# One weight chunk issued from ScalarE's queue, and two fewer warming products, at the start of a conditioned mixture-of-experts layer

## The chip, the cores and the metric

The kernel runs on one core of a Trainium2 chip. The metric is the device time of one execution in microseconds (us). The kernel before takes 261.87 us (median of 4 runs, 261.02 to 262.16).

## The reference

For 64 sequences of 64 rows of 512 values, a condition scales the rows, one layer follows, and then a base layer with a shared and a routed low-rank part; the input is added at the end. All is float32.

```python
# B=64 sequences, N=64 rows, D=512; condition q: (64, 256); E=6 experts of rank R=16, TOP_K=2
q_emb = relu(q @ W3 + b3)                              # (64, 512)
v     = (N * x + x.sum(axis=1, keepdims=True)) * q_emb[:, None, :]
y     = relu(v @ W2 + b2)

base   = y @ W_base + b_base
shared = (y @ A_s) @ B_s
gates  = softmax(y @ W_router + b_router)              # (…, 6)
w      = gates kept only at its TOP_K largest, else 0
routed = sum over e of ((y @ A_r[e]) * w[e]) @ B_r[e]
out    = x + base + shared + routed
```

## The kernel before

The 512 features lie on the partitions in four chunks of 128 (index `c`), the rows on the free axis. The 4096 rows are taken in four blocks (`k`) of 1024, each of two halves of 512 columns. In each block, the scaled input v goes through W2 (`py`, `yx`, `yy`, `yw`, `yz`, later `ia`, `ib`), then y through the concatenated low-rank and router weights (`ph`), then through W_base and the low-rank outputs (`ox`, `oy`, `oz`, `ow`, `last`). Most of the large products are written as Strassen-like sums of blocks, whose operand sums VectorE forms (`t`, `s`, `inner_t`, `tb`).

The order of instructions on each engine is the order of the source; there is no planner. Each engine has one queue, in order. DMAs are issued by SyncE's queue (SP), apart from two small stores at the very end that ScalarE issues (line 663).

What the change touches is the start of block 0:

- **Loads.** SP issues, in this order: `head` (condition, biases and W3's first output chunk, 198 KB, line 105), the first half of x's chunk 0 (`load_xa(0)`, 128 KB, line 100), W2's rows of chunk 0 (`load_w2(0)`, 256 KB, line 103), the second half of x's chunk 0 (`load_xa(1)`), the rest of W3 (384 KB, line 110), and then, for the chunks 1 to 3 in turn, x's first half (line 97), W2's rows, and the other half of x. The views call W3 and W2 together `w_sb`.
- **ScalarE's first instruction** is an activation of one column, `scratch` (line 106). Ahead of a kernel's first activation ScalarE loads its table of functions (ACT_TABLE_LOAD, shown under line 106).
- **TensorE's first instructions** are products of ones with ones in bf16 (`idle`, line 181): their result is never read. `first_mixed` runs eight, then the condition's product for output chunk 0 (`embed([0])`, `pq`, line 187), and two more products of ones.
- **The first scaled rows.** `embed` ends on ScalarE with the relu that gives `q_sb` (line 191). `modulate_group` works on VectorE: sums over each sequence (`vsum`, line 228), 64 x plus the sum (line 238, two instructions), times `q_sb` (line 242). The first quarter of block 0's chunk 0 then goes through W2 on TensorE (`part`, line 354, tile `py`, eight instructions), followed by `embed` for the three other chunks (twelve instructions) and then by the next quarter and the chunks 1, 2 and 3.
- **The second half of each chunk** is scaled on ScalarE (`modulate_scalar`, lines 247 to 250) and enters `yx` (line 361) and the sums of rows `s` (lines 263 to 266) that the products `yy`, `yw` and `yz` (line 170) take.

A float32 product is two instructions on TensorE in the views.

Of the kernel before, what the change touches and what calls it, by code (L numbers as in the profile page):

```python
# [15 lines left out]
P = 128  # L16
# [20 lines left out]
def adaln_ffn(ctx: ExitStack, tc: tile.TileContext, xa, x0, x1, head, w3, w2, wb, a, bcat, br, outT):  # L37
# [8 lines left out]
    nc = tc.nc  # L46
# [12 lines left out]
    def temps(name):  # L59

        return {n: tmp.tile([P, KH, TB], F32, tag=n, name=f"{n}_{name}") for n in pair_tags}

    def load_x(k):
        xs[k] = xpool.tile([P, NC, 2, TB], F32, tag="x", name=f"x_{k}")
        for c in CHUNKS:
            nc.sync.dma_start(xs[k][:, c].rearrange("p h t -> p (h t)"), x1[k, c])
# [24 lines left out]
    w2_sb = const.tile([P, NC, D], F32, tag="w2_sb", name="w2_sb")  # L91
# [7 lines left out]
    def load_xa(n):  # L99
        nc.sync.dma_start(xs[0][:, 0, ts(n, TB // 2)], xa[n])  # L100

    def load_w2(c):
        nc.sync.dma_start(w2_sb[:, c, :], w2[ts(c, P), :])

    nc.sync.dma_start(head_sb, head)
    nc.scalar.activation(scratch, ones[:, :1], AF.Relu)
    load_xa(0)
    load_w2(0)
    load_xa(1)
    nc.sync.dma_start(w3_sb, w3)  # L110
    for c in range(1, NC):
        load_x0(c, 0)
        load_w2(c)
        load_x0(c - 1, 1)
# [63 lines left out]
    def idle(n):  # L178
        p = ps_p.tile([P, TB], F32, tag="pp", name="idle")
        for _ in range(n):  # L180
            nc.tensor.matmul(p, ones[:, :P], ones, start=True, stop=True)

    def embed(fs, name):
        pq = ps_h.tile([P, len(fs), B], F32, tag="ph", name=name)
        for n, f in enumerate(fs):
            for c in range(NQ):
                nc.tensor.matmul(
                    pq[:, n], w3_of[f][:, c], cond_sb[:, c, :], start=(c == 0), stop=(c == NQ - 1)
                )
        for n, f in enumerate(fs):  # L190
            nc.scalar.activation(q_sb[:, f, :], pq[:, n], AF.Relu, bias=b3_sb[:, f : f + 1])
# [38 lines left out]
    def modulate_group(v, vsum, c, lo, hi):  # L230

        nb = hi - lo
        batch_sums(vsum, c, lo, hi)
        xc = batches_of(c, lo, hi)
        vc = v[:, c, :, lo * NH : hi * NH].rearrange("p h (b n) -> p h b n", n=NH)
        sc = vsum[:, c, lo:hi]
        for h in range(2):
            nc.vector.scalar_tensor_tensor(
                vc[:, h], xc[:, h], float(N), sc.unsqueeze(2).to_broadcast([P, nb, NH]), ALU.mult, ALU.add
            )  # L240
        q = q_sb[:, c, lo:hi].unsqueeze(1).unsqueeze(3).to_broadcast([P, 2, nb, NH])
        nc.vector.tensor_tensor(vc, vc, q, ALU.mult)

    def modulate_scalar(v, vsum, nq, c, lo, hi):

        batch_sums(vsum, c, lo, hi)
        nc.vector.tensor_scalar(nq[:, c, lo:hi], q_sb[:, c, lo:hi], float(N), None, ALU.mult)
        nc.vector.tensor_tensor(vsum[:, c, lo:hi], vsum[:, c, lo:hi], q_sb[:, c, lo:hi], ALU.mult)  # L248
        for b in range(lo, hi):
            nc.scalar.activation(  # L250
                v[:, c, :, ts(b, NH)], batches_of(c, b, b + 1)[:, :, 0], AF.Identity,
                bias=vsum[:, c, b : b + 1], scale=nq[:, c, b : b + 1],
            )

    def row_sums(a, name, cols=slice(0, TB)):

        all_s = mid.tile([P, 4, KH, TB], F32, tag=name, name=name)
        s = [all_s[:, i, :, cols] for i in range(4)]
        a11, a12, a21, a22 = a[:, :KH, 0, cols], a[:, KH:, 0, cols], a[:, :KH, 1, cols], a[:, KH:, 1, cols]

        def steps(c=slice(0, KH)):
            return [
                lambda: nc.vector.tensor_tensor(s[0][:, c], a21[:, c], a22[:, c], ALU.add),
                lambda: nc.vector.tensor_tensor(s[1][:, c], s[0][:, c], a11[:, c], ALU.subtract),
                lambda: nc.vector.tensor_tensor(s[2][:, c], a11[:, c], a21[:, c], ALU.subtract),
                lambda: nc.vector.tensor_tensor(s[3][:, c], a12[:, c], s[1][:, c], ALU.subtract),
            ]

        return {1: a11, 2: a12, 3: s[3], 4: a22, 5: s[0], 6: s[1], 7: s[2], "sums": all_s}, steps
# [3 lines left out]
    def fill(n):  # L273
        for _ in range(min(n, len(behind))):
            for step in behind.pop(0):
                step()
# [62 lines left out]
    def relu(y, f, h, src, cols=slice(0, TB)):  # L339
        nc.scalar.activation(y[:, f, h, cols], src, AF.Relu, bias=b2_sb[:, f : f + 1])  # L340

    def first_mixed(y):

        vs[0] = v = xpool.tile([P, NC, 2, TB], F32, tag="x", name="v_0")
        vsum = small.tile([P, NC, BB], F32, tag="vsum", name="vsum_0")
        nq = small.tile([P, NC, BB], F32, tag="nq", name="nq_0")
        half, cols = BB // 2, BB // 2 * NH
        other = slice(cols, TB)  # L350
        s, s_steps = row_sums(v, "s", other)

        def part(p, c, f, lo, hi):
            nc.tensor.matmul(  # L354
                p[:, :, lo * NH : hi * NH], w2_sb[:, c, ts(f, P)], v[:, c, :, lo * NH : hi * NH],
                start=(c == 0 and lo == 0), stop=(c == NC - 1), skip_group_check=True,
            )

        def without_sums(c):
            for j in range(KH):  # L360
                nc.tensor.matmul(  # L361
                    px[:, j], w2_sb[:, c, ts(j, P)], v[:, c, 0, other],
                    start=(c == 0 and j == 0), stop=(c % KH == KH - 1),
                    skip_group_check=True,
                )

        idle(8)
        embed([0], "pq0")
        idle(2)
        p0 = [ps_p.tile([P, 2, cols], F32, tag="pp", name=f"py_{f}") for f in range(NC)]  # L370

        px = ps_p.tile([P, KH, cols], F32, tag="pp", name="yx_0")
        p1 = mid.tile([P, KH, cols], F32, tag="p1", name="p1_0")
        for c in range(NC):
            pieces = ((0, half // 2), (half // 2, half)) if c == 0 else ((0, half),)
            for lo, hi in pieces:
                modulate_group(v, vsum, c, lo, hi)
                for f in range(NC):
                    part(p0[f], c, f, lo, hi)
                if c == 0 and lo == 0:  # L380
                    embed(range(1, NC), "pq")
            if c > 0:
                modulate_scalar(v, vsum, nq, c - 1, half, BB)
            if c == KH:
                for n in range(KH):
                    without_sums(n)
        nc.scalar.copy(p1, px)
        modulate_scalar(v, vsum, nq, NC - 1, half, BB)
        for f in range(NC):
            nc.scalar.activation(y[:, f, :, :cols], p0[f], AF.Relu, bias=b2_sb[:, f : f + 1])  # L390
        for c in range(KH, NC):
            without_sums(c)
        load_x(2)
        for step in t2_steps + inner_steps[:4] + s_steps():
            step()
        prepare(1, tb_steps + inner_steps[4:])
        fill(1)
        pairs = temps(0)
        for j in range(KH):
            relu(y, j, 0, px[:, j], other)  # L400
        banks = [ps_p.tile([P, KH, cols], F32, tag="pp", name=f"y{n}_0") for n in "ywz"]
        for j in range(KH):
            f1, f2 = j, KH + j
            temp = lambda n: pairs[n][:, j, :cols]
            py, pw, pz = (p[:, j] for p in banks)
            u, r, r1, r2 = temp("u"), temp("u22"), temp("u21"), temp("u12")
            product(py, 6, j, t2, s, start=j == 0)
            nc.vector.tensor_tensor(u, py, p1[:, j], ALU.add)
            product(pw, 5, j, t2, s, start=j == 0)
            nc.vector.tensor_tensor(r, pw, u, ALU.add)  # L410
            product(pz, 7, j, t2, s, start=j == 0)
            nc.vector.tensor_tensor(r, pz, r, ALU.add)  # L412
            relu(y, f2, 1, r, other)
            fill(1)
            product(pw, 3, j, t2, s, start=False)
            nc.vector.tensor_tensor(r2, pw, u, ALU.add)
            relu(y, f2, 0, r2, other)
            fill(1)
            product(pz, 4, j, t2, s, start=False)
            nc.vector.tensor_tensor(r1, pz, u, ALU.add)  # L420
            relu(y, f1, 1, r1, other)
            fill(1)
# [415 lines left out]
```

## Time and profile before

| | us |
|---|---|
| median of 4 runs (range) | 261.87 (261.02 to 262.16) |
| the profiled execution's own time | 261.66 |
| its span in the profile | 259.9 |
| TensorE busy (PE) | 254.9, 98% of the span |
| VectorE busy (DVE) | 193.8, 75% |
| ScalarE busy (ACT) | 136.5, 53% |
| GpSimd busy (POOL) | 38.7, 15% |
| bytes moved | 28.54 MB, mean 110 GB/s |

The span is the time from the first to the last record of the profiled execution; the execution's own time is 1.76 us longer. Starts are given in us from the start of the span. A busy share is an average over the whole span: the first microseconds, where the loads arrive, look different from the rest. PEld is TensorE's weight load, which overlaps with the products. "<-" in brackets names what ended the wait before an instruction.

### The profile page before, as it was taken

To read this page: it belongs to the slowest core of one execution; us is meant where nothing else is said; L and a number is where in the kernel's file an instruction comes from. 1 tells how busy PE (TensorE), PEld (TensorE's weight loads), DVE (VectorE), ACT (ScalarE), POOL (GpSimd) and SP (SyncE) were. 2 spreads that over 40 slices of the span, in tenths; PEclk is the share of its full clock that TensorE was granted. 3 is DMA by queue.
4 is the path that set the end of the run, shared out by engine and by line. 5 is a ranking of instruction groups with operands and counts; after the bars stand their busy time and mean duration, and the time that the engine had idled before them with its cause. 6 is when DMAs were issued, how large, how long until landed. Compare 5 with 4: busy or idle time off the path is not lost.

```text
span 259.9 us, 3177 instructions
## 1 busy us (share of the span) xinstructions
PE 254.9 (98%) x1004; PEld 164.5 (63%) x1004; DVE 193.8 (75%) x386; ACT 136.5 (53%) x373; POOL 38.7 (15%) x53
## 2 busy tenths in 40 slices
PE   7999999999999999999999999999999999999995
PEld 3756896454478888444458889544447889745453
DVE  2899898799968967968995894987895475872332
ACT  2399496596047896289017889349404428112000
POOL 1000000020017610002005630002001770000100
PEclk9999999999999999999999999999999999999999
DMA  6997639403320044000521024200332022400233
GB/s 210 381 342 261 268 105 374 166 3 121 121 81 0 13 154 161 0 3 2 199 82 42 0 83 164 81 0 3 121 121 81 0 79 89 159 0 3 75 140 108
DMA packets 14145, 28.54 MB, mean 110 GB/s; under 512 B 1472, under 2 KB 2496, under 8 KB 14128
## 3 DMA queue, kind: packets, MB, share of 16 engines
q1 hardware_dynamic: 13840, 28.21, 30.5%
q8 instruction: 8, 0.13, 0.2%
q10 hardware_dynamic: 288, 0.13, 0.2%
q14 instruction: 9, 0.07, 0.1%
HBM read 19.94 MB, written 8.39 MB: 109 GB/s over the span
## 4 chain that ended last, share of the span: by engine, by line
PE 94%; ACT 2%; DMA 2%; SPq 0%; issue 0%; DVE 0%
PE ia L446 13%; PE ph L779 11%; PE oz L170 11%; PE ox L170 11%; PE ib L446 10%; PE ow L170 9%; PE py L354 5%; PE oy L170 5%; PE ow L641 5%; PE ox L641 3%; PE oz L641 3%; DMA w_sb<-in_w_dram 2%; PE yw L170 1%; PE pt L704 1%; PE last L650 1%; PE yx L361 1%
## 5 line engine op out<-in xcount | busy, mean ns | idle before, releaser
L212 ACT ACTIVATE x<-x,vsum,nq 128x64 f32<-128x64 f32 x192 | 67.5, 431 | 7.0 <-DVE vsum L208 7.0
L779 PE MATMUL ph<-a_sb,y 128*128 128x118 f32 x256 | 30.5, 276 | 0.3 <-ACT y L340 0.3
L779 PEld LDWEIGHTS ph<-a_sb,y 128*128 128x128 f32 x256 | 30.0, 192 | 1.2 <-ACT y L340 0.7
L437 DVE TENSOR_TENSOR u<-ib,u 128x256 f32<-128x256 f32 x42 | 16.4, 418 | 18.5 <-PE ib L446 18.3
L452 ACT COPY ib<-ia 128x256 f32<-128x256 f32 x21 | 7.6, 361 | 42.3 <-PE ia L446 42.3
L170 PE MATMUL ox<-y,wb_sb 128*128 128x512 f32 x64 | 29.5, 593 | 0.0
L708 POOL TENSOR_TENSOR hwd<-hwT 112x512 f32<-112x512 f32 x4 | 5.8, 1452 | 136.3 <-ACT hwT L706 136.3
L170 PEld LDWEIGHTS ox<-y,wb_sb 128*128 128x128 f32 x64 | 11.9, 190 | 13.4 <-issue 13.2
L437 DVE TENSOR_TENSOR u<-ia,u 128x256 f32<-128x256 f32 (+1 forms) x36 | 16.1, 461 | 2.9 <-ACT u L484 1.6
L446 PE MATMUL ib<-inner_s,inner_t 128*128 128x256 f32 x60 | 17.8, 384 | 0.0
L340 ACT ACTIVATE y<-u,head_sb 128x256 f32<-128x256 f32 (+1 forms) x30 | 15.8, 585 | 3.8 <-DVE u L412 3.1
L637 DVE SCALAR_TENSOR_TENSOR xu<-oz,head_sb,xu 128x512 f32<-128x512 f32 x16 | 12.0, 749 | 7.2 <-PE oz L170 4.8
L207 DVE TENSOR_REDUCE vsum<-x 128x8 f32<-128x512 f32 x24 | 16.2, 675 | 0.0
L170 PE MATMUL oz<-sy,tb 128*128 128x512 f32 x32 | 15.2, 599 | 0.0
L170 PE MATMUL oz<-y,tb 128*128 128x512 f32 x32 | 15.1, 592 | 0.0
L170 PE MATMUL oy<-sy,tb 128*128 128x512 f32 x32 | 15.0, 592 | 0.0
L354 PE MATMUL py<-v,w_sb 128*128 128x512 f32 (+1 forms) x40 | 14.4, 510 | 0.6 <-DMA w_sb<-in_w_dram 0.6
L170 PE MATMUL ow<-sy,tb 128*128 128x512 f32 x28 | 13.2, 592 | 0.0
L170 PE MATMUL ow<-sy,wb_sb 128*128 128x512 f32 x28 | 13.2, 591 | 0.0
L455 ACT COPY ib<-ib 128x256 f32<-128x256 f32 x21 | 7.6, 363 | 9.9 <-PE ib L446 9.9
L446 PEld LDWEIGHTS ib<-inner_s,inner_t 128*128 128x128 f32 x60 | 11.2, 190 | 2.2 <-ACT ib L455 0.8
L250 ACT ACTIVATE v<-x,vsum,nq 128x64 f32<-128x64 f32 x32 | 11.0, 428 | 1.7 <-DVE vsum L248 1.7
(173 smaller groups left out, 461.9 us busy)
## 6 DMA issues: line engine op xcount, KB each, us to landing
xu<-in_x_dram SPq DMA_DIRECT2D x16, 512.0 KB, 4.3
out_dram<-xu SPq DMA_DIRECT2D x30, 256.0 KB, 2.0
x<-in_x_dram SPq DMA_DIRECT2D x12, 512.0 KB, 7.6
x<-in_x_dram SPq DMA_DIRECT2D x7, 256.0 KB, 5.4
w_sb<-in_w_dram SPq DMA_DIRECT2D x4, 256.0 KB, 5.3
wb_sb<-in_wb_dram SPq DMA_DIRECT2D x4, 256.0 KB, 5.0
w_sb<-in_w_dram SPq DMA_DIRECT2D x1, 384.0 KB, 4.9
out_dram<-xu SPq DMA_DIRECT2D x2, 192.0 KB, 1.9
```

What stands on the lines that cost most here:

```text
L170: nc.tensor.matmul(ps, w[i][:, c, ts(j, P)], s[i][:, c, :], start=start and c == 0, stop=c == KH - 1, skip_group_check=True,)
L207: nc.vector.tensor_reduce(vsum[:, c, bs], xc, AX.XY, ALU.add)
L212: nc.scalar.activation(x, x, AF.Identity, bias=vsum[:, c, b : b + 1], scale=nq[:, c, b : b + 1])
L250: nc.scalar.activation(v[:, c, :, ts(b, NH)], batches_of(c, b, b + 1)[:, :, 0], AF.Identity, bias=vsum[:, c, b : b + 1], scale=nq[:, c, b ...
L340: nc.scalar.activation(y[:, f, h, cols], src, AF.Relu, bias=b2_sb[:, f : f + 1])
L354: nc.tensor.matmul(p[:, :, lo * NH : hi * NH], w2_sb[:, c, ts(f, P)], v[:, c, :, lo * NH : hi * NH], start=(c == 0 and lo == 0), stop=(c = ...
L437: add = lambda o, a, b: nc.vector.tensor_tensor(o, a, b, ALU.add)
L446: nc.tensor.matmul(bank[b, t][:, cols], t_side(o, n), s_side(o, n), start=n == 1, stop=True, skip_group_check=True,)
L452: nc.scalar.copy(bank["b", t][:, lo], bank["a", t][:, lo])
L637: nc.vector.scalar_tensor_tensor(t, ps[name, j], bb_sb[:, f : f + 1], t, ALU.add, ALU.add)
L641: nc.tensor.matmul(ps[name, j], bcat_sb[:, ts(f, P)], hw, start=False, stop=True, skip_group_check=True)
L779: nc.tensor.matmul(ph[:, h * NS + s, :HC], y[:, c, h, ts(s, P)], a_sb[:, c, :], start=(c == 0), stop=(c == NC - 1),)
```

## The change

W2's chunk 0 is no longer issued third by SP. ScalarE's queue issues it, as its first instruction, ahead of the activation of `scratch` and so ahead of the table load. SP's other loads keep their order. The number of products of ones ahead of the condition's product goes from eight to six; the two behind it stay.

```diff
-    def load_w2(c):
-        nc.sync.dma_start(w2_sb[:, c, :], w2[ts(c, P), :])
+    def load_w2(c, queue=nc.sync):
+        queue.dma_start(w2_sb[:, c, :], w2[ts(c, P), :])
 
     nc.sync.dma_start(head_sb, head)
+    load_w2(0, nc.scalar)
     nc.scalar.activation(scratch, ones[:, :1], AF.Relu)
     load_xa(0)
-    load_w2(0)
     load_xa(1)
...
-        idle(8)
+        idle(6)
         embed([0], "pq0")
         idle(2)
```

## The prediction, written before the change was run

> **What bounds the kernel now.** I read the page first, then the chain of waits in order of time, then the timeline of the first 16 us, then single tiles. The page's chain says which engine carries the span:
>
> ```profile
> PE 94%; ACT 2%; DMA 2%; SPq 0%; issue 0%; DVE 0%
> ```
>
> TensorE carries it, so a gain at the start survives only if TensorE still has it when it later meets another engine with no slack. The start of the chain (start, length, what):
>
> ```profile
> 0.74 0.38 SPq L105
> ...
> 1.18 0.42 SPq L100
> ...
> 1.64 4.48 DMA w_sb<-in_w_dram
> ...
> 6.26 1.96 PE py L354 x8
> 8.22 1.28 PE pq L187 x12
> ```
>
> The first products on x (py) start at 6.26, released by W2's first chunk: issued third on SP's queue at 1.64, landed at 1.64 + 4.48 = 6.12. The change aims at this. The timeline (start, length, engine, line) shows what is late next:
>
> ```profile
> 0.73 1.28 ACT L106 ACT_TABLE_LOAD   x1 [0.73 <-PEq L824]
> 0.77 3.57 PE L181 MATMUL idle<-const-bfloat16-1.0 128*128 128x512 bf16 x8 [0.77 <-PEq L824]
> ...
> 3.61 0.42 DVE L228 TENSOR_REDUCE vsum<-x 128x4 f32<-128x256 f32 x1 [3.61 <-DMA x<-in_xa_dram]
> 3.71 1.19 PEld L187 LDWEIGHTS pq<-head_sb 128*128 128x128 f32 x4 [0.28 <-issue]
> ...
> 4.14 0.95 PE L187 MATMUL pq<-head_sb 128*128 128x64 f32 x4
> ...
> 5.13 0.31 ACT L191 ACTIVATE q_sb<-pq,head_sb 128x64 f32<-128x64 f32 x1 [2.90 <-PE pq L187]
> ...
> 5.47 0.42 DVE L242 TENSOR_TENSOR v<-v,q_sb 128x256 f32<-128x256 f32 x1 [0.92 <-ACT q_sb L191]
> ...
> 8.14 0.69 DVE L228 TENSOR_REDUCE vsum<-x 128x8 f32<-128x512 f32 x1 [0.22 <-DMA x<-in_x_dram]
> ...
> 9.54 0.72 ACT L191 ACTIVATE q_sb<-pq,head_sb 128x64 f32<-128x64 f32 x3 [4.11 <-PE pq L187]
> 9.89 0.69 DVE L242 TENSOR_TENSOR v<-v,q_sb 128x512 f32<-128x512 f32 x1 [0.27 <-ACT q_sb L191]
> ```
>
> The scaled x (v) is ready at 5.47 + 0.42 = 5.90, only 0.22 before W2. It hangs on the condition's product (4.14), which stands behind the eight products of ones. From 8.14 on VectorE hardly rests; its one wait there is 0.27 at 9.89, for q_sb from products that come after py. Does VectorE have slack later? The timeline around 24 us:
>
> ```profile
> 24.94 1.10 PE L170 MATMUL yy<-s,t 128*128 128x256 f32 x4
> ```
>
> Those products need the sum of L264, which VectorE starts at 24.10 and ends 0.69 later, at 24.79. Slack is about nothing, so what reaches the end is what VectorE gains at 9.89.
>
> **The change part by part.**
>
> *ScalarE's queue.* W2's issue takes some 0.42 (SP's rows at 1.18 and 1.64) ahead of the table load: the load moves from 0.73 to 1.16 and ends at 2.44, the activation of `scratch` (0.20) at 2.64. ScalarE's next work is at 5.13; this costs nothing while those 2.5 us cover it. Without that cover it would cost 0.42.
>
> *SP's queue.* Every SP issue behind the head chunk and the first half of xa moves up by one place, 2.11 - 1.64 = 0.47. Whether the landings follow is open, because the engines are 93 to 104% busy from 2 to 8 us (346 GB/s at 4 to 6): bounds 0 and 0.47. The ones that matter are x at L228 (wait 0.22, landed 8.12) and W3 (issued 2.58, 4.9 to land, 7.4 to 7.5, used at 7.84). Call this d2; I take at least 0.1, toward the low end, since a busy engine gains nothing from an earlier issue.
>
> *W2 itself.* Issued at 0.73 with the same 4.48 it lands at 5.21; with the 198 KB of the head beside it, 198/346 = 0.57 later, 5.78. Either is before 5.90.
>
> *The head chunk.* It now shares the DMA engines with W2's 256 KB: delay d1 between 0 (head first) and 256/346 = 0.74 (W2 first), as far as bytes go. The trace's packet records add a far end: W2's first packets took 0.33 to 0.66 on eleven occasions and 1.3 and 1.6 on two, where 0.084 is usual, so the ceiling is 0.74 + 1.60 = 2.34. I take 0.37, the middle of the byte bounds, because two queues of about equal size are likely to take turns. The first half of xa may be delayed likewise, but its reduce and two following steps end at 4.55 and L242 starts at 5.47: 0.92 of cover.
>
> *Six products of ones.* They start every 0.427, so two free 0.85; but the head lands at 0.74 + 2.5 = 3.24 (3.28 for its last part), so the weight load at 3.71 can move only to about 3.28 + 0.11 = 3.39 (0.11 is what lay between W2's landing and the load after it). Its first product stood 0.43 behind it because the last product of ones was still running; unobstructed, 0.15 to 0.33. The condition's product moves by 0.42 to 0.60; I take 0.50, before d1.
>
> *The clock.* The weight loads of the condition take 333 ns until 4.57 and 190 ns from 6.33; the trace's clock record has the full clock from 5.16, though the page's row of the clock shows 9 in every slice. Fewer ones leave TensorE a gap of about (3.39 + d1) - 3.33 ahead of the condition. I cost it at nothing: the two products of ones behind the condition, and a gap of 0.64 that the kernel already had at 5.62, lie around it. If the step to full clock is missed, the eight py products double from 1.73 to 3.46.
>
> Sum. The condition moves 0.50 - 0.37 = 0.13 earlier: v at 5.77, py at 5.77 + 0.14 = 5.91 instead of 6.26, a gain of 0.35. The weights of the twelve pq products load 1.58 after py (7.84 against 6.26), so at 7.49; W3, at 7.4 with d2 = 0.1, does not hold them. So q_sb at 9.54 and L242 at 9.89 gain 0.35 if x lets them: L228 can give 0.27 + d2, enough from d2 = 0.08. After that VectorE, ScalarE (back to back from 17.44) and TensorE at 24.94 move by the same 0.35. In the profiled execution's own time: 261.66 - 0.35 = 261.31. That execution lies 0.21 under the median of 261.87, so against the median 261.5.
>
> Two rules speak against more. The Trainium skill, "DMA: Bandwidth & Descriptors", section "Issuing engines are not separate DMA queues", says that transfers from different issuing engines run on the same 16 DMA engines, so a second queue saves only issue time. By that rule the gain in bytes is zero (d2 = 0, a gain of 0.27) where my bounds have 0 to 0.47; no row here shows SP's and ScalarE's loads sharing at the start. "TensorE: Matmul & The Clock Gate", Part 1, says that the clock is released by a free-running window of 3.4 us of activity, not by a count of products; by it a missed window would hold py at half speed and cost up to 1.7, against my zero.
>
> **The rivals.**
>
> *A, the head comes first and all issues count (faster).* d1 = 0 moves the condition by 0.42 to 0.60, v to 5.30 to 5.48, py to 5.44 to 5.62: 0.64 to 0.82. L242 follows if d2 is 0.45 or more, that is if nearly all of the 0.47 reaches the landings. Time 261.87 - 0.75 = 261.1. For: W2's wait does end last at 6.26. Against: DMA engines at 93 to 104%.
>
> *B, the head stands behind W2 on the DMA engines (slower).* Place: the landing of head_sb, which gates the product at 4.14. From d1 = 0.50 + 0.22 = 0.72 on, py starts later than now, and each further us goes one for one through q_sb (no slack at 9.89). With W2's bytes first (0.74) and a slow packet of about 1 us, d1 is 1.74 and the loss 1.0: 262.9. The ceiling of 2.34 loses 1.6: 263.5. It passes 0.3% when the head lands after 3.28 + 1.51 = 4.8. TensorE then also idles over 1.5 us before the clock step. For: W2's slow first packets, now beside the head. Against: SP's head issue is no later than ScalarE's.
>
> *C, the table load still goes first.* Then W2 is issued at 2.02 or later, lands from 6.50, py starts at 6.64: 0.4 lost, 262.3.
>
> **How the numbers follow.** Forecast 0.34, A 0.29, B 0.32, C 0.05. A difference of 0.3% (0.79 us) is about what a measurement of this kernel can tell from no change: 261.08 to 262.66. The forecast's own range is 261.1 to 261.9 (d1 from 0 to 0.74 at a move of 0.50: gain 0.72 to 0), all inside the 0.3%. A straddles the border: 0.25 faster, 0.04 inside. B: 0.30 slower, 0.02 inside. C is inside. Together 0.25 faster, 0.45 same, 0.30 slower. The range for 8 in 10 reaches down to 260.7 (A's best, 261.87 - 0.82 = 261.05, less about 0.35, since single runs of before stand between 0.85 under and 0.29 over their median) and up to 262.9, which leaves out the upper half of B.
>
> **What would show it.** Right: a first packet of W2 before 2 us on ScalarE's queue, the condition's first product at 3.9 to 4.1, py at 5.8 to 6.0 released by VectorE and no longer by W2, L242 of the second chunk at 9.5 to 9.6, the products on s at 24.6. Wrong: a reduce of the first half of xa after 4.3, a condition's product after 4.6 released by the head (B), weight loads of 333 ns still in py (a missed clock), or L228 at 8.1 with the wait of 9.89 gone (x as the bound, gain at most 0.27).

## The result

The changed kernel takes 262.73 us in the median of 54 runs (261.26 to 263.57); before takes 261.64 in 78 runs over the same time. The ratio is 1.0031, with a 95% interval of 1.0024 to 1.0039: slower, by about the 0.3% that the prediction named as the border. The means are 262.52 and 261.69, 0.82 apart; the medians lie 1.09 apart. The median hides the shape. The 54 times fall into two groups with nothing between 261.77 and 262.32: 13 runs from 261.26 to 261.77, and 41 from 262.32 to 263.57. The 78 runs of before lie in one group up to 262.28, apart from two at 263.6.

The profiled execution of the change, 263.57 us with a span of 261.8, belongs to the upper group. Its page's chain still lies on TensorE:

```profile
PE 94%; ACT 2%; DMA 1%; DVE 1%; issue 0%; SPq 0%; DVEq 0%
```

The start of the chain of waits (start, length, what) no longer holds W2:

```profile
0.74 0.37 SPq L105
...
1.16 3.86 DMA x<-in_xa_dram
...
6.59 3.48 PE py L354 x8
10.06 1.28 PE pq L187 x12
```

W2 has left, and the first half of xa stands in its place. But py begins at 6.59 (6.26 before), and the same eight products take 3.48 us instead of 1.96. The timeline (start, length, engine, line, what, and in brackets the wait) shows the steps between:

```profile
0.73 0.41 ACTq L103 DMA_DIRECT2D w_sb<-in_w_dram  x1
...
0.77 2.72 PE L181 MATMUL idle<-const-bfloat16-1.0 128*128 128x512 bf16 x6 [0.77 <-PEq L824]
...
1.17 1.28 ACT L107 ACT_TABLE_LOAD   x1 [1.17 <-PEq L824]
...
4.41 1.12 PE L187 MATMUL pq<-head_sb 128*128 128x64 f32 x4 [0.92 <-DMA head_sb<-in_head_dram]
...
5.05 0.42 DVE L228 TENSOR_REDUCE vsum<-x 128x4 f32<-128x256 f32 x1 [5.05 <-DMA x<-in_xa_dram]
...
5.56 0.31 ACT L191 ACTIVATE q_sb<-pq,head_sb 128x64 f32<-128x64 f32 x1 [2.89 <-PE pq L187]
6.11 0.43 DVE L242 TENSOR_TENSOR v<-v,q_sb 128x256 f32<-128x256 f32 x1
...
6.59 3.48 PE L354 MATMUL py<-v,w_sb 128*128 128x256 f32 x8 [0.21 <-DVE v L242]
...
11.39 0.72 ACT L191 ACTIVATE q_sb<-pq,head_sb 128x64 f32<-128x64 f32 x3 [5.51 <-PE pq L187]
11.73 0.69 DVE L242 TENSOR_TENSOR v<-v,q_sb 128x512 f32<-128x512 f32 x1 [2.50 <-ACT q_sb L191]
```

The six products of ones are through at 3.49, the head chunk lands at 4.36 (3.28 before), and TensorE waits 0.92 us for it. The first half of xa lands late too, at 5.02 instead of 3.58, and it sets the start of py: q_sb is ready at 5.87, but L242 starts only at 6.11, 1.06 behind the start of xa's reduce, and this distance is 1.05 to 1.07 in every profile with W2 on ScalarE's queue. The L242 that decides is at 11.73 instead of 9.89, and the products on s behind it are late by the same amount:

```profile
26.77 1.10 PE L170 MATMUL yy<-s,t 128*128 128x256 f32 x4
```

26.77 - 24.94 = 1.83 of the 1.91 by which the two profiled executions differ (263.57 - 261.66). Of these, 0.33 is the later start of py and 3.48 - 1.96 = 1.52 its length. The view of the tile `w_sb` up to 12 us says why py is long (duration in ns as min/median/max):

```profile
L354 PEld LDWEIGHTS py<-v,w_sb x13: 190/338/338, 6.6 to 11.9; 128*128 128x128 f32 x13
```

These weight loads took 190 in the py of before; 338 is what they take at the lower clock (333 in the condition of before, ahead of the step). The trace's record of the clock gives full speed from 9.62 on, where the profile of before has 5.16. TensorE stepped up late and did nearly all of py at the lower clock, half of full speed by that record.

So there are two suspects, which came together: the clock (a rest of TensorE, a stretch without any product, ahead of the condition's product makes it miss the step: theory 1), and the bytes (the head and xa land late because W2 shares the DMA engines with them: theory 2). The products of ones might also count by their number (theories 3 and 4).

### The profile page after: what moved, and what is told of

It reads as the page before. It is cut to its first block, busy times and chain, and to the rows that moved or that the text cites. A ratio compares the mean times of both kernels' runs of the same rounds, so it can differ in the third digit from the quotient of the medians.

```text
span 261.8 us, 3173 instructions
## 1 busy us (share of the span) xinstructions
PE 256.3 (98%) x1002; PEld 165.2 (63%) x1002; DVE 193.7 (74%) x386; ACT 136.5 (52%) x373; POOL 38.7 (15%) x53
## 4 chain that ended last, share of the span: by engine, by line
PE 94%; ACT 2%; DMA 1%; DVE 1%; issue 0%; SPq 0%; DVEq 0%
PE ia L446 13%; PE ph L779 11%; PE oz L170 11%; PE ox L170 11%; PE ib L446 10%; PE ow L170 9%; PE py L354 6%; PE oy L170 5%; PE ow L641 5%; PE ox L641 3%; PE oz L641 3%; DMA x<-in_xa_dram 1%; PE yw L170 1%; PE pt L704 1%; PE last L650 1%; PE yx L361 1%
## 5 line engine op out<-in xcount | busy, mean ns | idle before, releaser
L354 PE MATMUL py<-v,w_sb 128*128 128x512 f32 (+1 forms) x40 | 15.9, 555 | 0.2 <-DVE v L242 0.2
L354 PEld LDWEIGHTS py<-v,w_sb 128*128 128x128 f32 x40 | 8.5, 218 | 6.7 <-issue 4.8
```

What stands on the lines that cost most here:

```text
L354: nc.tensor.matmul(p[:, :, lo * NH : hi * NH], w2_sb[:, c, ts(f, P)], v[:, c, :, lo * NH : hi * NH], start=(c == 0 and lo == 0), stop=(c = ...
```

## Experiments

**One half of the change each, and a gap without the queue.** The first keeps W2 on ScalarE's queue with eight products of ones; the next two keep SP's queue with six and with four.

```diff
# e1_queue_only, against the change        # e2_six_only (e3_four_only: 4), against before
-        idle(6)                             -        idle(8)
+        idle(8)                             +        idle(6)
```

> W2's first chunk on ScalarE's queue as in the change, but eight products of ones as before. Theory 1 (the clock: the 0.92 us in which TensorE waits for the head is what makes it miss the step to the full clock): the eight products end at 4.2 instead of 3.3, the wait for the head shrinks to some 0.2 us, the clock steps up before the products py in nearly all executions, and the time is 261.2 to 261.6, 0.998 to 1.000 of before. Theory 2 (the bytes: the head lands 1.1 us late, and everything behind it is late): the head still lands at about 4.4, and the time stays at 262.5 to 263, 1.003 to 1.005 of before.

> W2's first chunk on SyncE's queue as before, six products of ones. Theory 1 (the gap before the condition): the head lands at 3.3 as the six products end, the gap is about 0.1 us, no step of the clock is missed, and the condition's product comes some 0.4 us earlier but py still waits for W2 at 6.1: 261.4 to 261.7, 0.999 to 1.001. Theory 3 (the number of products of ones by itself): as the change, 262.5 to 263, 1.003 to 1.005. Theory 2 (late bytes): no loss, as theory 1.

> W2's first chunk on SyncE's queue as before, four products of ones: the products end at 2.5 and the head lands at 3.3, so TensorE waits some 0.9 us ahead of the condition, as after the change, while every DMA is as before. Theory 1 (the clock): most executions miss the step and lose 1.0 to 1.7 us: 262.3 to 263.3, 1.003 to 1.006. Theory 2 (late bytes): no loss, 261.4 to 261.7, 1.000.

| | median us (range, runs) | ratio to before (95%) |
|---|---|---|
| e1, ScalarE's queue, eight | 261.45 (261.39 to 261.79, 11) | 0.9987 (0.9978 to 0.9995) |
| e2, SP's queue, six | 262.83 (261.18 to 263.54, 12) | 1.0024 (1.0006 to 1.0042) |
| e3, SP's queue, four | 262.73 (262.32 to 263.69, 7) | 1.0038 (1.0022 to 1.0053) |

The queue alone is faster, in one narrow group. Six products alone are as slow as the change, with no DMA touched. Theory 2 expected the reverse in both. But theory 1 in the form I gave it missed e2 too: I had looked only at the rest ahead of the condition. The timeline of e2, TensorE alone:

```profile
3.28 1.05 PE L187 MATMUL pq<-head_sb 128*128 128x64 f32 x4
4.12 1.06 PE L181 MATMUL idle<-const-bfloat16-1.0 128*128 128x512 bf16 x2
6.18 3.75 PE L354 MATMUL py<-v,w_sb 128*128 128x256 f32 x8 [0.99 <-DMA w_sb<-in_w_dram]
```

There is no rest ahead of the condition, as I expected; the rest has moved behind it, 0.99 us until W2 lands. The clock steps up at 10.14 and py takes 3.75. In e3 the rest ahead of the condition is 0.61, and the step comes at 8.33. In e1, by contrast (TensorE, and VectorE's L242 that decides):

```profile
4.14 0.91 PE L187 MATMUL pq<-head_sb 128*128 128x64 f32 x4
4.88 0.60 PE L181 MATMUL idle<-const-bfloat16-1.0 128*128 128x512 bf16 x2
5.93 1.99 PE L354 MATMUL py<-v,w_sb 128*128 128x256 f32 x8 [0.45 <-DVE v L242]
...
9.60 0.69 DVE L242 TENSOR_TENSOR v<-v,q_sb 128x512 f32<-128x512 f32 x1 [0.67 <-ACT q_sb L191]
```

The head lands at 3.80 here, while the eight products still run; the condition starts at 4.14 as before, the clock steps up at 4.88, and py starts at 5.93 instead of 6.26, released by VectorE.

**W2 behind the table load.**

```diff
# e4_after_table, against the change
-    load_w2(0, nc.scalar)
     nc.scalar.activation(scratch, ones[:, :1], AF.Relu)
+    load_w2(0, nc.scalar)
```

> W2's first chunk on ScalarE's queue, but behind the table load and the activation of scratch, six products of ones. Its issue moves to about 2.2, so its packets no longer stand beside the head's. Theories 1 and 2 alike: the head lands at 3.3 to 3.5, no gap, the clock steps up in time; W2 lands between 5.2 and 6.3, and the time is 261.2 to 261.8, 0.998 to 1.000. If the head is late here too (two queues sharing is not its cause), 262.5 or more.

262.68 us (261.45 to 263.54, 12 runs), ratio 1.0028 (1.0009 to 1.0047). The expectation failed at its first step. The timeline:

```profile
0.73 1.28 ACT L106 ACT_TABLE_LOAD   x1 [0.73 <-PEq L824]
...
0.79 0.38 ACTq L103 DMA_DIRECT2D w_sb<-in_w_dram  x1
```

ScalarE's sequencer issued the DMA at 0.79, during the table load ahead of it; only the engine was held. "Ahead of the table" in the change is therefore worth 0.06 us, and e4 is the change over again: the head at 3.65, six products, the clock's step at 9.33. It does not tell whether W2 causes the head's delay.

**The same number of products in other places.**

```diff
# e5_six_four, against before              # e6_queue_six_four, against the change
-        idle(8)
+        idle(6)                                     idle(6)
         embed([0], "pq0")                           embed([0], "pq0")
-        idle(2)                             -        idle(2)
+        idle(4)                             +        idle(4)
```

> W2's first chunk on SyncE's queue as before; six products of ones ahead of the condition and four behind it (before: eight and two). Theory 1 (rests of TensorE inside one window of the clock's monitor): the two moved products fill the rest of about 1 us that six alone left between the condition and py; TensorE works nearly without a rest from 0.8 to 5.8, the clock steps up by 7.6 at the latest, 261.2 to 261.8, 0.998 to 1.001. Theory 3 (the number of products ahead of the condition): slow as with six and two, 262.5 to 263.3, 1.002 to 1.006.

> W2's first chunk on ScalarE's queue; six products of ones ahead of the condition and four behind it. The total of ten is that of before, but the rest of some 1 us ahead of the condition, while TensorE waits for the head, stays. Theory 1 (rests): most executions still miss the step, 262.4 to 263.6, 1.002 to 1.006 (the two added products can also put py back by up to 0.4). Theory 4 (the total number of products of ones before py): 261.3 to 261.9, 0.998 to 1.001.

| | median us (range, runs) | ratio to before (95%) |
|---|---|---|
| e5, SP's queue, six and four | 261.66 (261.16 to 262.76, 12) | 0.9999 (0.9984 to 1.0013) |
| e6, ScalarE's queue, six and four | 263.01 (261.37 to 263.67, 12) | 1.0035 (1.0015 to 1.0056) |

Both kernels run ten products of ones, six of them ahead. On SP's queue the four behind fill the rest; on ScalarE's queue TensorE waits ahead of the condition, where they cannot help. TensorE in the timelines, first of e5 and then of e6:

```profile
3.29 1.12 PE L187 MATMUL pq<-head_sb 128*128 128x64 f32 x4
4.21 1.33 PE L181 MATMUL idle<-const-bfloat16-1.0 128*128 128x512 bf16 x4
5.42 1.97 PE L354 MATMUL py<-v,w_sb 128*128 128x256 f32 x8
```

```profile
3.82 1.12 PE L187 MATMUL pq<-head_sb 128*128 128x64 f32 x4 [0.33 <-DMA head_sb<-in_head_dram]
4.73 1.91 PE L181 MATMUL idle<-const-bfloat16-1.0 128*128 128x512 bf16 x4
6.44 2.92 PE L354 MATMUL py<-v,w_sb 128*128 128x256 f32 x8
```

e5 has no rest and steps up at 4.80; e6 rests 0.33 by the records, less than the 1 us expected, and steps up at 8.51. Neither the number ahead (theory 3) nor the total (theory 4) decides: it is where TensorE rests.

**Between six and eight, and one more behind.** Both against the change: e7 runs eight and three, e8 seven and two.

```diff
# e7_queue_eight_three, against the change # e8_queue_seven, against the change
-        idle(6)                             -        idle(6)
+        idle(8)                             +        idle(7)
         embed([0], "pq0")                           embed([0], "pq0")
-        idle(2)                                     idle(2)
+        idle(3)
```

> W2's first chunk on ScalarE's queue; eight products of ones ahead of the condition, three behind it. Theory 1: the rest of 0.45 ahead of py, which the kernel with eight and two on this queue still had, is filled too; no step is missed, 261.2 to 261.6, 0.997 to 0.999. If the third product comes in py's way where the clock is still at half speed, up to 0.3 is lost again, 261.5 to 261.8.

> W2's first chunk on ScalarE's queue; seven products of ones ahead of the condition, two behind it. The rest ahead of the condition is between those of six (1.1) and eight (0.2 or less): some 0.1 to 0.6 as the head lands at 3.8 to 4.4. Theory 1: a mixture, some executions miss the step; the median lies between 261.4 and 262.6 and single ones reach from 261.2 to 263.3. Theory 2 (late bytes alone): one group of times, spread as before.

e7: 261.45 (261.37 to 261.81, 12 runs), ratio 0.9984 (0.9975 to 0.9993). e8: 261.51, with ten runs from 261.35 to 261.63 and two at 263.16 and 263.45, ratio 0.9996 (0.9979 to 1.0014). Seven products give a mixture, with fewer slow runs than six. e7 is level with e1 within the intervals. The added product did not fill the rest: in e7's profile py still waited 0.58 for VectorE, since xa landed at 4.53 and the step at 4.48 had shortened the added product. It bought nothing that these runs can tell from e1.

**The same kernel in both groups.** The change itself, three more single runs, each with its profile, beside a run of before at 261.47:

> The change itself once more, one look, to find an execution of the lower group of its times (13 of 54 executions lie at 261.3 to 261.8). Theory 1 (the clock): in such an execution the step to the full clock comes before 8.6 us, py takes about 2 us and not 3.5, and the time is 261.3 to 261.9; in one of the upper group the step comes after 8.6 and py takes 3 us or more. Theory 2 (late bytes): the groups differ in the landing of the head, and not in the clock.

> As the look before this one: the same kernel once more, with the same two groups of times and the same expectation of each theory for either group.

> As the two looks before this one: the same kernel once more, with the same two groups of times and the same expectation of each theory for either group.

They took 263.36, 261.59 and 262.95 us. The first two in the timeline, TensorE alone and then TensorE with the steps that release py:

```profile
4.05 1.12 PE L187 MATMUL pq<-head_sb 128*128 128x64 f32 x4 [0.55 <-DMA head_sb<-in_head_dram]
4.96 1.06 PE L181 MATMUL idle<-const-bfloat16-1.0 128*128 128x512 bf16 x2
6.12 3.73 PE L354 MATMUL py<-v,w_sb 128*128 128x256 f32 x8
```

```profile
4.04 0.66 PE L187 MATMUL pq<-head_sb 128*128 128x64 f32 x4 [0.55 <-DMA head_sb<-in_head_dram]
4.54 0.60 PE L181 MATMUL idle<-const-bfloat16-1.0 128*128 128x512 bf16 x2
4.56 0.42 DVE L228 TENSOR_REDUCE vsum<-x 128x4 f32<-128x256 f32 x1 [4.56 <-DMA x<-in_xa_dram]
...
4.74 0.31 ACT L191 ACTIVATE q_sb<-pq,head_sb 128x64 f32<-128x64 f32 x1 [2.07 <-PE pq L187]
...
5.62 0.42 DVE L242 TENSOR_TENSOR v<-v,q_sb 128x256 f32<-128x256 f32 x1
...
6.10 1.99 PE L354 MATMUL py<-v,w_sb 128*128 128x256 f32 x8 [0.96 <-DVE v L242]
```

In both, the head lands at 4.00, the rest is 0.55 and py starts within 0.02 us. The clock's step is at 9.66 in the one and at 3.54 in the other, py takes 3.73 or 1.99, and the times are 1.77 apart: 3.73 - 1.99 = 1.74 of it is py. Theory 2 is out as the cause of the two groups.

The third, 262.95, lies between them, and its step does too, at 8.81:

```profile
6.08 3.33 PE L354 MATMUL py<-v,w_sb 128*128 128x256 f32 x8
```

At half speed, half of the time from the start of py to the step is lost. That is (9.66 - 6.12) / 2 = 1.77 in the first and (8.81 - 6.08) / 2 = 1.37 in the third; against the second, their times are 1.77 and 1.36 longer. So the step's time accounts for the place within the upper group as well.

**What the profiles say of the clock's rule.** The clock's full-speed stretch is recorded as 256.00 or 252.59 us in each of the 13 profiles, and these differ by 3.41, a 75th of 256.00: the step goes by windows of 3.41 us. This is the window that the Trainium skill names ("TensorE: Matmul & The Clock Gate", Part 1), which it calls free-running, and the steps here do come at another phase in each execution. How full must the last window before the step be? Counting back 3.41 from each step, by TensorE's records:

| profile | time us | window that gave the step | rest in it | window before it | rest |
|---|---|---|---|---|---|
| before | 261.66 | 1.75 to 5.16 | 0.00 | | |
| e1 (eight) | 261.39 | 1.47 to 4.88 | 0.00 | | |
| e5 (six and four, SP) | 261.64 | 1.39 to 4.80 | 0.00 | | |
| e7 (eight and three) | 261.56 | 1.07 to 4.48 | 0.00 | | |
| e8 (seven) | 261.53 | 0.76 to 4.18 | 0.07 | | |
| change, second single run | 261.59 | 0.13 to 3.54 | 0.70 (0.65 at its start) | | |
| change | 263.57 | 6.21 to 9.62 | 0.21 | 2.80 to 6.21 | 0.92 |
| change, first single run | 263.36 | 6.25 to 9.66 | 0.00 | 2.84 to 6.25 | 0.66 |
| change, third single run | 262.95 | 5.39 to 8.81 | 0.10 | 1.98 to 5.39 | 0.51 |
| e2 (six, SP) | 263.54 | 6.73 to 10.14 | 0.00 | 3.32 to 6.73 | 0.99 |
| e3 (four, SP) | 262.40 | 4.91 to 8.33 | 0.44 | 1.50 to 4.91 | 0.61 |
| e4 (six, behind the table load) | 263.16 | 5.92 to 9.33 | 0.21 | 2.51 to 5.92 | 0.46 |
| e6 (six and four) | 262.83 | 5.10 to 8.51 | 0.00 | 1.69 to 5.10 | 0.33 |

Windows with no rest or little of it step up, and those with 0.92 or more do not. In between, the time of rest alone does not decide: 0.70 was enough in the second single run, where everything else was products of ones, and 0.44 in e3, but 0.33 was too much in e6. Every window in the last column also holds products of the condition, with 64 columns. That short products count for less would explain it; it was not tried by itself.

The phase explains the two groups. Six products of ones make a stretch of 2.7 us, and only a window that covers nearly all of it steps up in time; the next one ends 3.41 later. Where the border lies can be estimated. The shortest time of the upper group is 0.91 above the middle of the lower one (262.32 against 261.41), so its step came at about 6.1 + 2 x 0.91 = 7.9, in a window that followed one started at about 1.1. The window of the second single run started at 0.13 and stepped up; one of e2's that started at -0.10, just before the first record, did not. By this estimate windows that start between about 0.1 and 1.1 give the lower group, 1.0 of 3.41 or 29% of the phases if all are equally likely (not shown); 13 of 54 runs (24%) were in it.

With eight products there is hardly a rest after 0.77 as long as the clock is low. The condition starts at 4.14, and by the rows of the change the two products behind it start 0.91 later and take 1.06 at the lower clock, until 6.11; py follows at 6.26 in before. This is an estimate, since no profile here has eight products and a late step. By it the step comes at 6.9 at the latest and costs at most about 0.3, and 76 of the 78 runs of before do lie in one group. The two at 263.6 were not profiled.

## Why the prediction was wrong

The forecast was a gain of 0.35, 261.5 us; the change took 262.73, by the medians 1.09 more than before in the same stretch of runs. The stated range, 260.7 to 262.9, does hold 262.73, but by luck: its upper end was put there for rival B, a head so late that py waits for it, which did not happen.

- **The queue, right in its main part.** That W2 stops holding py, that VectorE releases it and that some 0.35 is gained is what e1 shows without the shorter row of products: py 0.33 earlier, L242 at 9.60 instead of 9.89, the products on s at 24.64 instead of 24.94, and 261.45 against 261.78, 0.33 less. The size agrees in part by chance: 0.13 of the 0.35 was to come from an earlier condition, which stands at 4.14 in e1 as before, and v is ready at 5.88 instead of 5.90; the gain is W2's alone. That VectorE's L242 carries the gain or loss to the end held in all 13 profiles: its shift from before and that of the span differ by at most 0.07.
- **The step that failed: the clock, costed at nothing.** I wrote that the two products behind the condition and "a gap of 0.64 that the kernel already had" lie around it. The gap of before lies behind a full window of products; the new one, and in e2 the one behind the condition, cuts the stretch that such a window needs. The prediction had priced a missed step right (3.46 - 1.73 = 1.73) but left it out of the sum. Measured, it is 1.74 on py with the same landings, and between 0.9 and 2.2 by where the step falls (the upper group against the middle of the lower one); it falls on 41 of 54 runs. The lower group, with 261.41 in the middle, gains as e1 does. Weight loads of some 333 ns in py, named as a sign of being wrong, are what the profile has.
- **Six products, credited with 0.50.** In e2 the condition did come earlier, 3.28 instead of 4.14, more than the 0.50. It bought nothing, because W2 came at 6.04, and it emptied the time before py.
- **d1, the head's delay, too small.** I took 0.37. The head landed at 3.65 to 4.36 in the profiles with ScalarE's queue and six products, against 3.28: 0.37 to 1.08. In the changed kernel it is 0.68 or more, and the rest ahead of the condition 0.51 to 0.92. With eight products it costs nothing, since the condition starts at 4.14 anyway.
- **xa's delay, put at nothing.** The prediction gave it 0.92 of cover. In the changed kernel xa landed 0.93 to 1.44 later than before, at 4.51 to 5.02, and used that up: in the second single run q_sb is ready at 5.05 and L242 starts at 5.62. So xa, not the condition, sets the start of py there, at 6.08 to 6.12 where the landings are earliest. Its reduce after 4.3 was the other sign of being wrong that came true. This makes the gain smaller; the loss is the clock's.
- **d2, too small.** The bounds were 0 to 0.47, because busy DMA engines were taken to gain little from an earlier issue. In e1 the x that L228 waits for landed 0.70 earlier (7.42 against 8.12); in the nine profiles with ScalarE's queue it landed at 6.89 to 8.13, in the four with SP's at 8.03 to 8.57. In these nine it gains nothing, since L242 waits for q_sb in each. With SP's queue x can be the bound: in e5 py starts at 5.42, yet L242 only at 9.81, behind x, and the time is that of before.
- **Rival B had the sign, and a late head, but not the path.** The head did come late; py started 0.33 later in the profiled execution, through xa, and 0.14 to 0.18 earlier than before in the three single runs (6.08 to 6.12). The loss that B asked of a late head came from the clock, which B mentioned only as a companion. Rival C did not occur, and e4 shows that it could not: there the DMA went out at 0.79, during the table load.
- **The two rules of the skill.** By the rule on issuing engines d2 was to be zero and the gain 0.27, near e1's 0.33, but not for that reason, as d2 shows. The rule on the clock, a free-running window, fits these profiles, and the "up to 1.7" that the prediction worked out for a missed window fits the 1.74 measured. I set it aside without asking how long the unbroken stretch of products must be for any phase.

What stays open: that W2's packets cause the head's delay is likely, since the head landed at 3.17 to 3.28 in every profile with W2 on SP's queue and at 3.65 or later in every one with ScalarE's; xa, issued at 1.16 to 1.18 in all of them, landed at 3.47 to 3.58 and at 4.38 or later. How the loads share the DMA engines was not tried by itself, nor what exactly makes the clock step up.

## What to carry to other kernels

Products that only warm TensorE are sized by the length of the unbroken stretch of work that they complete, not by when the first useful operand lands: the stretch has to hold a whole window at any phase. For a window of 3.41 us that takes nearly two windows of work without a long rest, of which the useful products may be a part, as py is here. Cutting the warming products, or letting a wait into the middle, costs half-speed work in some share of the executions. When a small change gives two groups of times, compare one profile of each group before explaining the median. Where a transfer is moved to another queue, look at what was first on the old queue, here the head and xa, and keep enough cover for those to land later.

## What the runs showed of the hardware

- In the second single run of the change, a window of 3.41 us with 0.70 of rest (80% busy, all of it products of ones) sufficed for the full clock; one of e2's that ended at 3.32, with 0.87 of rest at its start (74% busy), did not. In e6, 0.33 of rest was too much in a window that also holds the condition's products.
- A DMA issue that stands behind an activation on ScalarE's queue went out at 0.79 in e4, while the table load of 1.28 us ahead of it had only started at 0.73.
- With W2's 256 KB issued at the same time from ScalarE's queue, the head's 198 KB took 2.9 to 3.6 us from issue to landing, against 2.4 to 2.5 with W2 third on SP's queue. W2 itself took 3.2 to 3.9, against 3.6 to 4.5.
